# Layer 2 attention: head outputs in two halves of a PSUM bank, output products two runs later, projection weights in two buffers

## The chip, the cores and the metric

The kernel runs on one core of a Trainium2 chip. The metric is the device time of one execution in microseconds, the median of three runs. The profile is of one further execution, which has a time of its own.

## The reference

A stack of four layers works on x of shape (4, 256, 256) with a context of shape (4, 1601, 256), in float32. Each layer adds an attention part and a feed-forward part to x. The change is in the attention of layer 2, grouped-query attention with 16 query heads and 4 key/value heads of 128 values, over 1601 context positions and, causally, the 256 own ones:

```python
q = rms_norm((x @ wq).reshape(B, L, 16, 128), q_norm_w)
k = rms_norm((x @ wk).reshape(B, L, 4, 128), k_norm_w)
v = (x @ wv).reshape(B, L, 4, 128)
k_ctx = rms_norm((h_ctx_kv @ wk_ctx).reshape(B, T, 4, 128), k_norm_w)
v_ctx = (h_ctx_kv @ wv_ctx).reshape(B, T, 4, 128)
q = q * cos + rotate_half(q) * sin
k = k * cos + rotate_half(k) * sin
# keys and values: context first, then own; each repeated for 4 heads
scores = einsum('bhld,bhmd->bhlm', q, k_full) / sqrt(128) + mask
out = einsum('bhlm,bmhd->blhd', softmax(scores), v_full)
return out.reshape(B, L, 16 * 128) @ wo
```

It is applied to the layer-normalised x, and its result is added to x.

## The kernel before

The four layers run one after the other on one core. Work of a later stage is filled into gaps of an earlier one: the context's keys and values of layer 2 do not depend on x, and are computed ahead by a generator, `l2_early`. It makes products (L1307), copies them out of PSUM on ScalarE (L1314, L1315), normalises the keys on GpSimd (L1332), turns them with TensorE transposes (L1341), and stores them to DRAM (L1316 for values, L1344 for keys). `self.fill(n)` takes n steps of this generator; what is left when the attention's own preparation is through is run off by `for _ in self.early`.

`l2_xattn` works in 16 **units**: 4 batch entries times 4 key/value heads, each unit with 4 query heads, so 64 heads in all. For each unit, `prep` is a generator of small steps: on the first unit of a batch entry the layer norm and its transposes (`turned`, tile `tp_ln`, L1420); then the query products of the first 128 rows (`tpq`); the loads of the context's keys and values (kT, va) from DRAM, and the products for own keys and values (`tpkv`); the query products of the other 128 rows; the norms; the transposes of the queries (`tpqT`, L1526); and the transposes of the own keys (`tpk`, L1531), copied into kT (L1534). All these PSUM tiles have the tag "tp" in the pool `ps`, which has one buffer, so that each must be read before the next is written.

The weights of a unit, `wq` (128 x 1024 values a unit) and `wks` (128 x 512), are loaded by `load` (L1439), and its output weights `wo` (128 x 1024) by `load_out` (L1444); the loads are issued on the queue of SyncE (SP), in program order, together with those of keys and values and the early stores. `one` is a pool with one buffer for each tile, `two` has two.

The main loop counts **runs** x, 16 in a unit and 4 in a head, and takes three at a time (`pos` 0, 1, 2). A run is one of four chunks of a head: 16 score matmuls (L117, tile s), the mask and the maximum on VectorE (L1568, L1571), and the exponentials on ScalarE (L1576). The scores of three runs are issued together. Twelve runs later than its scores, a chunk of the value products of a head is done (`value_chunk`): a quarter of the 15 key tiles, accumulated in the PSUM tile `o2`, which `ps_o` holds with one buffer. After the last chunk of a head, ScalarE copies `o2` into `at` (L1631). Meanwhile the probabilities have been merged (`merge`), scaled on GpSimd (L1611) and turned on VectorE (L1617).

`beside(n, k)` says what else stands behind run k of unit n: the steps of the preparation of the next unit (k = 1, 3, 7, 9, 12) and of the one after it (k = 15, and k = 13 too where that one begins a new batch entry), the loads of weights (k = 3) and of output weights (k = 12), and `project` at k = 11. `project` does the output products of the unit before: 8 matmuls of `at` with `wo` into the PSUM tile `acc2` (tag "tp"), which show as 16 records, and VectorE adds the result to x (L1639). Its fourth head's value products have just ended at k = 11, since they come twelve runs late.

In this loop the order on TensorE is that of the program: `self.strict` pins each matmul behind the one before. The order on the other engines is largely that in which the program issues the work. An instruction waits for the semaphores of the tiles that it reads or overwrites.

Of the kernel before, what the change touches and what calls it, by code (L numbers as in the profile page):

```python
# [11 lines left out]
F32 = mybir.dt.float32  # L12
# [12 lines left out]
P = 128  # L25
B = 4
S = 256
# [22 lines left out]
REGS = 4  # L50
F1 = [1, 2, 2, 3]
G1 = [7, 4, 4, 3, 2, 2, 2, 2, 2, 2, 0]
LN2, Q2, C2 = 2, 2, 6
FIRST3 = [7, 1, 3]
EARLY = B * NKV2
NH3, HD3 = 32, 8
# [41 lines left out]
class Kernel:  # L98
# [1262 lines left out]
    def l2_xattn(self):  # L1361
# [10 lines left out]
        with ExitStack() as es:  # L1372
            one = es.enter_context(tc.tile_pool(name="a2one", bufs=1, reuse_waits="tile"))
            two = es.enter_context(tc.tile_pool(name="a2", bufs=2, reuse_waits="tile"))
            ps_s = es.enter_context(tc.tile_pool(name="a2s", bufs=3, space=PSUM))
            ps = es.enter_context(tc.tile_pool(name="a2p", bufs=1, space=PSUM))
            ps_o = es.enter_context(tc.tile_pool(name="a2o", bufs=1, space=PSUM))
# [57 lines left out]
            def load(g):  # L1435
                w = {}
                for n, shape in (("wq", [P, 2, 512]), ("wks", [P, 2, 256])):
                    w[n] = one.tile(shape, F32, name=n)
                    nc.sync.dma_start(w[n], i["l2_" + n][g])  # L1439
                return w  # L1440

            def load_out(g):
                t = two.tile([P, 4, D], F32, name="wo")
                nc.sync.dma_start(t, i["l2_wo"][g])  # L1444
                return t
# [176 lines left out]
            def values(va, pT, at, h, o, ms):  # L1622
                for m in ms:
                    n0 = {13: 1, 14: 5}.get(m, 0)
                    rows = 96 if m == 14 else P
                    self.mm(
                        o[:, 32 * n0 :].rearrange("p (n i) -> p n i", i=32), va[:rows, m, :],
                        pT[:rows, n0:, m, :], m == 0, m == CT,
                    )
                if ms[-1] == CT:  # L1630
                    nc.scalar.copy(at[:, h, :], o)  # L1631

            def project(hd):
                b, at, wo = hd["b"], hd["at"], hd["wo"]
                acc = ps.tile([P, 2, D], F32, name="acc2", tag="tp")
                for q in range(2):
                    for h in range(4):
                        self.mm(acc[:, q, :], at[:, h, q * P : (q + 1) * P], wo[:, h, :], h == 0, h == 3)
                nc.vector.tensor_tensor(self.x[b], self.x[b], acc, ALU.add)  # L1639

            ORDER = [0, 13, 14, *range(1, NM)]
            CHUNK = [ORDER[0:4], ORDER[4:8], ORDER[8:12], ORDER[12:]]

            def value_chunk(hd, n):
                if n == 0:
                    hd["o"] = ps_o.tile([P, S], F32, name="o2")
                values(hd["va"], hd["pT"], hd["at"], hd["h"], hd["o"], CHUNK[n])

            units = [(b, g) for b in range(B) for g in range(NKV2)]
            w = load(0)  # L1650
            wo = load_out(0)
            results = {0: []}
            for n, _ in enumerate(prep(0, w, results[0])):
                self.fill(Q2 if n == 0 else C2 if n == 3 else 0)
            for _ in self.early:
                pass
            w = load(1)
            self.es2.close()
            main = es.enter_context(tc.tile_pool(name="a2main", bufs=2, side="right", reuse_waits="tile"))

# [12 lines left out]
            def prepare(n):  # L1673

                if n < len(units):
                    if n not in pieces:
                        pieces[n] = prep(n, w, results.setdefault(n, []))
                    next(pieces[n], None)

            def beside(n, k):  # L1680

                nonlocal w, wo
                if k == 11 and n:
                    project(heads[4 * n - 1])
                if k in (1, 3, 7, 9) or (n, k) == (0, 0):
                    prepare(n + 1)
                if k == 12:
                    for _ in range(2):
                        prepare(n + 1)
                    if n + 1 < len(units):  # L1690
                        wo = load_out(units[n + 1][1])
                if k == 3 and n + 2 < len(units):
                    w = load(units[n + 2][1])
                if k == 15 or (k == 13 and (n + 2) % NKV2 == 0):
                    prepare(n + 2)
# [13 lines left out]
            for x0 in range(0, ALL + LATE, 3):  # L1709
                made, norms = [], False  # L1710
                for x in range(x0, min(x0 + 3, ALL)):
                    if x % 16 == 0:
                        begin(x // 16)
                    hd = heads[x // 4]
# [14 lines left out]
                for pos in range(3):  # L1729
                    x = x0 + pos  # L1730
                    if LATE <= x < ALL + LATE:
                        value_chunk(heads[(x - LATE) // 4], (x - LATE) % 4)
                    if pos == 0:
                        soften(made[2:])
                    if x < ALL:
                        beside(x // 16, x % 16)
                        norms |= x % 16 == 4
                    if pos == 0:
                        for hd in turning:
                            turns(hd)  # L1740
# [768 lines left out]
```

## Time and profile before

| what | value |
| --- | --- |
| median of 3 runs | 2410.82 us (2408.73 to 2413.48) |
| the profiled execution: its time | 2415.17 us |
| the profiled execution: span on the core | 2413.5 us |
| mean granted TensorE clock | 0.969 |
| first score matmul of layer 2 | 701.06 us |
| last output copy of a head, L1631 | 1709.8 us |

Times in the trace are microseconds from the start of the span. PE is TensorE, PEld its loading of weights, DVE is VectorE, ACT ScalarE, POOL GpSimd and SP SyncE, which only issues transfers; SPq is its queue. A row of a group names the source line, the engine, the operation, output <- inputs, the shapes and the number of instructions, and then the busy time, the mean of one in ns, and the idle time of the engine just before them with what ended most of it. A row of the timeline gives the start, the duration, and the instruction with its number; idle time before it stands in brackets, with what released it. Matmul ends are modelled, so that chains of matmuls overlap by some 0.16 us.

### The profile page before, as it was taken

To read this page: it belongs to the slowest core of one execution; us is meant where nothing else is said; L and a number is where in the kernel's file an instruction comes from. 1 tells how busy PE (TensorE), PEld (TensorE's weight loads), DVE (VectorE), ACT (ScalarE), POOL (GpSimd) and SP (SyncE) were. 2 spreads that over 40 slices of the span, in tenths; PEclk is the share of its full clock that TensorE was granted. 3 is DMA by queue.
4 is the path that set the end of the run, shared out by engine and by line. 5 is a ranking of instruction groups with operands and counts; after the bars stand their busy time and mean duration, and the time that the engine had idled before them with its cause. 6 is when DMAs were issued, how large, how long until landed. Compare 5 with 4: busy or idle time off the path is not lost.

```text
span 2413.5 us, 42181 instructions
## 1 busy us (share of the span) xinstructions
PE 2249.5 (93%) x14322; PEld 1389.0 (58%) x14335; DVE 1506.1 (62%) x3586; ACT 1267.4 (53%) x2871; POOL 950.4 (39%) x1707
## 2 busy tenths in 40 slices
PE   8989997899978999999999999999899889999996
PEld 5677875777744655555555555555765533444332
DVE  5453532673457877887877878878434484758344
ACT  3234443452455545554555545554232477888994
POOL 1014654502325554554555455455112244334220
PEclk9999998889999999999999999999899999999998
DMA  7164575652541111111111111100434254434320
GB/s 264 41 199 158 169 152 151 201 185 64 165 167 37 51 42 51 51 48 49 51 51 51 51 50 38 51 23 1 196 112 128 86 167 119 101 100 99 84 63 19
DMA packets 156078, 234.47 MB, mean 97 GB/s; under 512 B 33929, under 2 KB 122761, under 8 KB 154666
## 3 DMA queue, kind: packets, MB, share of 16 engines
q1 hardware_dynamic: 138998, 190.07, 24.8%
q0 software_dynamic: 11280, 31.60, 5.4%
q10 hardware_dynamic: 5588, 10.09, 1.4%
q8 instruction: 117, 1.92, 0.3%
q14 instruction: 95, 0.78, 0.1%
HBM read 169.94 MB, written 61.74 MB: 96 GB/s over the span
## 4 chain that ended last, share of the span: by engine, by line
PE 65%; DVE 18%; ACT 6%; issue 6%; DMA 2%; POOL 2%; SPq 0%; another core or an unknown queue 0%; ACTq 0%; PEld 0%; POOLq 0%; DVEq 0%; PEldq 0%
PE o L117 11%; PE s L117 10%; PE o L77 7%; DVE pT L1617 4%; PE b L77 3%; DVE nmsm L1571 3%; PE f2gu L117 3%; ACT p L1576 3%; PE s L77 3%; PE f1gu L117 2%; PE f0gu L117 2%; PE fill L1307 2%; PE acc L117 2%; PE av L117 2%; PE f0y L117 2%
## 5 line engine op out<-in xcount | busy, mean ns | idle before, releaser
L1576 ACT ACTIVATE p<-s,nmsm 128x448 f32<-128x448 f32 (+2 forms) x512 | 323.5, 638 | 347.2 <-DVE nmsm L1571 205.8
L117 PE MATMUL o<-pT,va 128*128 128x256 f32 (+2 forms) x1920 | 433.4, 376 | 14.0 <-ACT at L1631 13.0
L77 ACT ACTIVATE e<-s 128x1024 f32<-128x1024 f32 (+1 forms) x416 | 392.3, 1042 | 58.6 <-PE s L77 57.6
L117 PEld LDWEIGHTS o<-pT,va 128*128 128x128 f32 (+1 forms) x1920 | 345.1, 190 | 126.2 <-issue 64.9
L117 PE MATMUL s<-kT,qT 128*32 128x448 f32 (+2 forms) x4096 | 414.3, 552 | 2.6 <-ACT p L1576 2.6
L1611 POOL TENSOR_SCALAR p<-p,rm 128x448 f32<-128x448 f32 (+2 forms) x512 | 321.8, 651 | 6.3
L1571 DVE TENSOR_REDUCE nmsm<-s 128x1 f32<-128x448 f32 (+4 forms) x384 | 298.8, 785 | 7.4 <-DVE s L1568 0.2
L1617 DVE STREAM_TRANSPOSE pT<-p 128x448 f32<-128x448 f32 (+4 forms) x384 | 275.7, 773 | 4.9 <-POOL p L1611 4.9
L117 PEld LDWEIGHTS s<-kT,qT 128*32 128x32 f32 x4096 | 124.5, 110 | 251.4 <-issue 227.5
L77 PE MATMUL o<-e,va 128*32 128x512 f32 x1656 | 248.0, 617 | 14.1 <-DVE os L77 12.2
L77 PEld LDWEIGHTS s<-qb,kb 32*128 32x128 f32 (+1 forms) x1664 | 65.6, 181 | 182.5 <-issue 143.0
L1568 DVE TENSOR_TENSOR s<-s,mask 128x64 f32<-128x64 f32 (+4 forms) x384 | 92.5, 255 | 93.3 <-PE s L117 61.8
L1604 POOL TENSOR_TENSOR rm<-em,tot 32x8 f32<-32x8 f32 x256 | 50.1, 196 | 227.1 <-DVE tot L1601 205.7
L522 POOL DMA_INDIRECT f0xr<-f0xd,f0src x95 | 90.8, 955 | 69.0 <-PE f0gu L117 17.4
L1307 PE MATMUL fill<-wkc_early,ctxT 128*128 128x256 f32 (+1 forms) x444 | 109.5, 398 | 6.8 <-ACT va_early L1315 4.1
L77 PE MATMUL s<-qb,kb 32*128 32x256 f32 (+1 forms) x1664 | 111.5, 331 | 2.6 <-ACT e L77 1.8
L77 POOL CAST kb<-kf 128x384 fp32r<-128x384 f32 (+1 forms) x126 | 65.6, 549 | 97.8 <-PE s L77 51.1
L1576 ACT ACTIVATION_READ_ACCUMULATOR p<-s,nmsm 128x1 f32 x512 | 101.5, 198 | 0.0
L1307 PEld LDWEIGHTS fill<-wkc_early,ctxT 128*128 128x128 f32 (+1 forms) x444 | 86.1, 198 | 22.4 <-ACT va_early L1315 5.2
L1326 DVE TENSOR_REDUCE ss_early<-sq_early 128x4 f32<-128x512 f32 x64 | 37.2, 581 | 85.0 <-ACT sq_early L1325 65.4
L630 POOL DMA_INDIRECT f0yt<-f0yd,f0slot x64 | 62.3, 974 | 62.3 <-DVE x L622 30.7
L117 PE MATMUL f2gu<-f2wgu,f2xsT 128*128 x176 | 84.3, 603 | 0.9 <-issue 0.6
(579 smaller groups left out, 3733.9 us busy)
## 6 DMA issues: line engine op xcount, KB each, us to landing
kf<-kd SPq DMA_DIRECT2D x384, 48.0 KB
vd<-va_early SPq DMA_DIRECT2D x96, 128.0 KB
kd<-kT_early SPq DMA_DIRECT2D x48, 256.0 KB
kT<-kd SPq DMA_DIRECT2D x16, 768.0 KB
va<-vd SPq DMA_DIRECT2D x16, 768.0 KB
kd<-kt SPq DMA_DIRECT2D x96, 128.0 KB
f0yd<-f0ys SPq DMA_DIRECT2D x95, 128.0 KB
ctxT<-in_ctxT SPq DMA_DIRECT2D x5, 1664.0 KB
```

The source lines that it names most:

```text
L77: ins = f(*a, **kw)
L117: self.ordered(self.nc.tensor.matmul(out, lhsT, rhs, start=start, stop=stop, **kw))
L522: nc.gpsimd.indirect_dma_start(out=t, out_offset=None, in_=xd[:, :], in_offset=bass.IndirectOffsetOnAxis(ap=src[:, n : n + 1], axis=0),)
L630: nc.gpsimd.indirect_dma_start(out=yt, out_offset=None, in_=yd[:, :], in_offset=bass.IndirectOffsetOnAxis(ap=slot[:, t, r : r + 1], axis=0),)
L1307: ins = nc.tensor.matmul(tp[:rows, t, :], ctxT[u // NKV2][:, k, c0 : c0 + rows], w[u % NKV2][:, k, :], start=k == 0, stop=k == 1,)
L1326: nc.vector.tensor_reduce(ss[:, m0:m1], sq[:, : m1 - m0, :], AX.X, ALU.add)
L1568: nc.vector.tensor_tensor(sv, sv, mask[:, e0:e1, : nt - CT, :].rearrange("p n t i -> p n (t i)"), ALU.add)
L1571: nc.vector.tensor_reduce(ms[:, 0, e0:e1], s[:, n0:n1, : nt * 32], AX.X, ALU.max, negate=True)
L1576: nc.scalar.activation(p[:, n, : nt * 32], s[:, n, : nt * 32], AF.Exp, bias=ms[:, 0, e : e + 1], accum_out=ms[:, 1, e : e + 1],)
L1604: nc.gpsimd.tensor_tensor(r[32 * a : 32 * a + 32], e[:, a], tot, ALU.mult)
L1611: nc.gpsimd.tensor_scalar(p[:, n, : nt * 32], p[:, n, : nt * 32], r[:, e : e + 1], 1.0, ALU.mult, ALU.mult)
L1617: self.pin(nc.vector.transpose(pT[:, 2 * c + n0 : 2 * c + n1, :nt, :].rearrange("p n t i -> p n (t i)"), p[:, n0:n1, : nt * 32],))
```

## The change

There are three parts.

1. The tile `o2` is allocated once, with room for two heads (128 x 2 x 256 values, 2 KB in each partition), and successive heads use its two halves in turn. Before, each head allocated a tile of 128 x 256 from the pool of one buffer.
2. `project` is called at k = 13, no longer at k = 11: two runs later.
3. `wq` and `wks` come from the pool with two buffers. With it the start of the layer is rewritten: the weights of the second unit are loaded right after the first step of the first preparation, ahead of the output weights, where they were loaded after all of the early work. The fill steps between the steps of the first preparation are 2, 1, 1, 0, 4; they were 2 after the first and 6 after the fourth.

```diff
-LN2, Q2, C2 = 2, 2, 6
+LN2, Q2 = 2, [2, 1, 1, 0, 4]
...
                 for n, shape in (("wq", [P, 2, 512]), ("wks", [P, 2, 256])):
-                    w[n] = one.tile(shape, F32, name=n)
+                    w[n] = two.tile(shape, F32, name=n)
                     nc.sync.dma_start(w[n], i["l2_" + n][g])
...
+            results = {}
+
             def value_chunk(hd, n):
                 if n == 0:
-                    hd["o"] = ps_o.tile([P, S], F32, name="o2")
+                    hd["o"] = outs[:, hd["h"] % 2, :]
                 values(hd["va"], hd["pT"], hd["at"], hd["h"], hd["o"], CHUNK[n])
 
             units = [(b, g) for b in range(B) for g in range(NKV2)]
+            outs = ps_o.tile([P, 2, S], F32, name="o2")
             w = load(0)
+            first = prep(0, w, results.setdefault(0, []))
+            next(first)
+            w = load(1)
             wo = load_out(0)
-            results = {0: []}
-            for n, _ in enumerate(prep(0, w, results[0])):
-                self.fill(Q2 if n == 0 else C2 if n == 3 else 0)
+            for n in Q2:
+                self.fill(n)
+                next(first)
+            for _ in first:
+                pass
             for _ in self.early:
                 pass
-            w = load(1)
             self.es2.close()
...
             def beside(n, k):
 
                 nonlocal w, wo
-                if k == 11 and n:
+                if k == 13 and n:
                     project(heads[4 * n - 1])
```

## The prediction

> **What bounds the kernel now.** I read the busy times first, then the stretches of this layer, then who waits for the lines that the change touches, then the timeline at two places.
>
> ```profile
> span 2413.5 us, 42181 instructions
> PE 2249.5 (93%) x14322; PEld 1389.0 (58%) x14335; DVE 1506.1 (62%) x3586; ACT 1267.4 (53%) x2871; POOL 950.4 (39%) x1707
> L117 PE MATMUL o<-pT,va 128*128 128x256 f32 (+2 forms) x1920 | 433.4, 376 | 14.0 <-ACT at L1631 13.0
> ```
>
> The next view has, by stretch: us, then the busy time of PE, PEld, DVE, ACT and POOL, the granted TensorE clock, the DMA share, GB/s.
>
> ```profile
> 660.00:701.00 41.00, 27.61 (x129) 20.11 (x127) 27.16 (x82) 23.40 (x58) 15.01 (x18) 0.94 0.62 207
> 747.00:1713.00 966.00, 946.61 (x6410) 571.50 (x6410) 757.98 (x1591) 482.77 (x1353) 490.77 (x1088) 1.00 0.13 43
> ```
>
> The 64 heads of this layer are worked off between 747 and 1713, and there TensorE is busy for 946.6 of 966 us: any TensorE idle time added or removed there is added to or taken from the end. The stretch from 660 to 701 is the start of the layer: 41.0 less 27.6 us leaves 13.4 us of idle TensorE. Next, who waits for the copy of a head's output out of PSUM (L1631):
>
> ```profile
>   PE o L117: 13.0, 15
>   PE acc L117: 3.2, 4
> ```
>
> So 13.0 us are lost by 15 heads' first value products and 3.2 us by 4 output products. The timeline shows what else stands around that copy:
>
> ```profile
> 804.71 1.46 PE L117 MATMUL acc<-wo,at 128*128 128x256 f32 x6
> 806.96 2.43 PE L117 MATMUL acc<-wo,at 128*128 128x256 f32 x10 [0.80 <-ACT at L1631]
> 809.23 1.63 PE L117 MATMUL o<-pT,va 128*128 128x256 f32 x8
> ...
> 866.45 3.62 PE L117 MATMUL acc<-wo,at 128*128 128x256 f32 x16
> 869.90 1.63 PE L117 MATMUL o<-pT,va 128*128 128x256 f32 x8
> 873.49 0.44 PE L1531 MATMUL tpk<-ident,ko 128*128 128x128 f32 x2 [1.95 <-DVE x L1639]
> 873.85 6.53 PE L117 MATMUL s<-kT,qT 128*32 128x448 f32 x48
> ```
>
> The output products (acc, 16 records a unit) stand exactly between a head's last value product and the next head's first. They are work to do while ScalarE copies: heads 0 to 2 of a unit are read first, only the fourth waits.
>
> **The change part by part.** (1) *Halves of one bank.* The wait of 13.0 us would go if a head's first product no longer needed the copy of the head before. But both halves are parts of one tile in one 2 KB bank, and in the changed program as built the first value product of every head still waits for the ScalarE copy of the head just before it. At the unit boundaries, where it waited for acc alone, it now names that copy as well. I take 0 for the 16.2 us; the bound below is −16.2, the bound above is 0 by itself.
>
> The trace alone, one buffer and a wait of 0.4 to 1.6 us each, would let one think that the wait is about the same bytes, and would give −13.0. [...]
>
> (2) *Output products two runs later* (k 11 to 13). This moves 15 groups of 16 matmul records and with each the VectorE addition L1639; no DMA is issued by it. A group takes 869.90 − 866.45 = 3.45 us. In its new place it does the same work, but the copy it covered is bare. The runs go in threes, so the 15 units m fall into classes:
> - m = 1, 4, 10, 13: the copy ends 2.03 us after the last product (by its rows, 804.87 to 806.91 at m = 1), ScalarE being in exponentials. Before: 809.23 − 804.87 = 4.36 us from the last product of one head to the first of the next, acc included. After: 2.08 of waiting, and 3.45 elsewhere, 5.53: +1.17 each, +4.7. If the copy came at once, as in the next class, +2.5.
> - m = 2, 5, 8, 11, 14, and 7: the copy ends 0.41 us after. Before 869.90 − 866.62 = 3.28; after 0.45 + 3.45 = 3.90: +0.62 each, +3.7 for six.
> - m = 3, 6, 9, 12, 15: 48 score matmuls (some 4.8 us) stand there too and cover the copy of 0.41: 0. Without them 0.62 each.
>
> In its new place acc has the same PSUM slots ("tp") as what comes next. At m = 2, 6, 10 that is now the normalised input's transposes (tp_ln), directly after it; they must wait for L1639. That addition ends 0.72 us after acc when VectorE is free: 0.77 plus the overlap of 0.16 that a chain of matmuls has, +0.93 each, +2.8. Where VectorE is behind, as at m = 2 before (870.07 to 873.43), it is 3.36. Gone is the wait of 1.95 that the K transposes (tpk) have there: −2.1 with the overlap. Behind acc now waits tpk's copy to SBUF (0.3 to 1.3 us after tpk); 8 value products of 1.63 us stand between: 0. The addition comes two runs later on VectorE, ahead of the same transposes of probabilities, with 4 us to spare: 0. The wo load of the next unit waits for acc and starts some 4 us later on SP, where nothing is queued behind it for long; it is needed 16 runs later (60 us): 0.
>
> *Clock.* After the 1.95 us stall the granted clock reads 0.50 from 874 to 877, and the 48 score matmuls took 6.53 us against 4.77 at 752.23: −1.8 if that stall goes. After a stall of 1.58 us (from 1044.8) the clock reads 1.00. The four bare stalls of 2.08 lie beyond the row with the drop: between 0 and 4 × 1.8 = +7.2. One row is thin evidence, and I take half, +3.6.
>
> [...]
>
> Steady part: 4.7 + 3.7 + 2.8 − 2.1 − 1.8 + 3.6 = **+10.9 us**.
>
> (3) *Weights in two buffers, fills 2, 1, 1, 0, 4.* In the steady part it removes no wait, since a weight load is issued some twelve runs ahead already (issued at 685, used at 713): 0. At the start:
>
> ```profile
> 626.63 0.38 SPq L1439 DMA_DIRECT2D wq<-in_l_wq  x1
> 670.58 0.38 SPq L1444 DMA_DIRECT2D wo<-in_l_wo  x1
> 663.81 1.10 PE L1307 MATMUL fill<-wkc_early,ctxT 128*96 128x256 f32 x4 [2.55 <-ACT va_early L1315]
> 677.63 1.97 PE L117 MATMUL tpkv<-wks,xT 128*128 128x256 f32 x8 [3.38 <-issue]
> 697.81 3.33 PE L1341 MATMUL fill<-ident,kr_early 128*128 128x128 f32 x13 [3.52 <-POOL kr_early L1332]
> ```
>
> On SP the first two weight loads (768 KB) go from 626–629 to about 670, behind a store that waits for ScalarE, and the second two come up to them from 684: five loads in a row (wq and wo of 128 x 1024 f32, wks of half that: 2 MB), at the 241 and 287 GB/s of the windows 696–700 and 704–708 some 8 us, and the K and V loads are queued behind. On TensorE the first query product moves behind 13 transposes and 16 fill records, from 667.25 to 672–674, and the K/V product from 677.6 to 679–681: a loss of 0 to 3.6. The last two fill groups of products come ahead of the query transposes (1.26 us and a wait of 1.21 no longer precede them): the 3.52 us wait for POOL's normalised K ends up to 2.4 us earlier, and with 768 KB less under way at 626–650 the waits of 2.55 and 0.97 near 664 may go. Bounds −5.9 to +3.6; I take −1.5, since the wait at 697.8 ends last there.
>
> **Sum:** +10.9 − 1.5 = +9.4. On the profiled span, 2413.5 + 9.4 = 2422.9, and with the 1.7 us around it 2424.6. That run was 4.35 us above the median of three: **2420 us**.
>
> **The rivals.**
> - *Faster by the start.* Place: 660 to 701, with 13.4 us idle and a granted clock of 0.54 to 0.61 from 696 to 704 (8 us at some 0.6: 3 us). If all of it went and no stall cost clock, 7.3 − 16.4 = −9.1: 2402. It decides once the start gains over 12 (7.3 + 4.8), and over 16 with two drops. For it: less traffic, earlier products. Against it: the query chain becomes later, not earlier, and five loads now meet at 670. 0.08.
> - *The halves free the products*, and the built wait is met early: −16.2; without a wait part 2 costs only its tp_ln and tpk terms (2.8 − 2.1 − 1.8 = −1.1) and the start −1.5: 2410.8 − 18.8 = 2392. For it: the 13.0 us that L1631 holds up. Against it: the wait is in the program. 0.04.
> - *Nothing to be seen*: no clock drop at the stalls (+7.3), a start nearer its bound (−5): 2410.8 + 2.3 = 2413. For it: only one stall of this length was seen with a drop; against it: both would have to come together. 0.20.
> - *Forecast*: 0.68, its own range 2415.6 to 2429; the top has all four drops and the start at its worst (14.5 + 3.6 = 18.1: 2429).
>
> Under 0.2% (4.8 us) a measurement of this kernel can't be told from no change. Faster 0.12, same 0.20, slower 0.68. Range 2409 to 2429: it holds the forecast and nearly all of the third case, and leaves out the first two.
>
> **What would show it.** Right: the first value products wait for the copy in some 25 heads, about 24 us in all (13.0 + 4 × 2.08 + 6 × 0.45); acc waits no longer for it; gaps of about 2.08 at m = 1, 4, 10, 13; tp_ln waits on L1639 three times; the stall at 873 is gone; 747 to 1713 becomes 8 to 12 us longer. Wrong: value products that no longer wait for L1631, a start of the scores before 695, or clock readings of 1.00 behind all the 2.08 us stalls.

## The result, and the profile after

| | before | after |
| --- | --- | --- |
| median, us (6 runs each) | 2408.72 (2406.92 to 2413.48) | 2420.05 (2414.96 to 2421.10) |
| profiled execution, span, us | 2413.5 | 2418.2 |
| first score matmul of layer 2, us | 701.06 | 693.38 |
| last value product, us | 1709.74 | 1718.38 |
| the loop between them, us | 1008.68 | 1025.00 |
| idle TensorE in the loop, us | 29.66 | 41.68 |

The changed kernel is slower: the ratio is 1.0042 with a 95% interval of 1.0029 to 1.0054, 11.3 us on the medians.

The busy row and the row of the value products on the page of after:

```profile
span 2418.2 us, 42254 instructions
PE 2253.0 (93%) x14335; PEld 1389.2 (57%) x14335; DVE 1508.3 (62%) x3586; ACT 1266.7 (52%) x2871; POOL 947.1 (39%) x1707
...
L117 PE MATMUL o<-pT,va 128*128 128x256 f32 (+2 forms) x1920 | 438.6, 378 | 27.5 <-ACT at L1631 26.5
```

The value products' idle time behind the copy L1631 has gone from 13.0 to 26.5 us. Who waits for that copy (first line), and who waits for the addition L1639 (second):

```profile
  PE o L117: 26.5, 25
```

```profile
  PE tp_ln L1420: 3.2, 3
```

It is 25 heads where it was 15, the output products no longer stand in that list, and the transposes of the normalised input wait three times for the addition. The timeline of the two places shown of before:

```profile
795.95 1.56 PE L117 MATMUL o<-pT,va 128*128 128x256 f32 x6
799.55 1.74 PE L117 MATMUL o<-pT,va 128*128 128x256 f32 x8 [2.04 <-ACT at L1631]
801.13 0.38 PE L1531 MATMUL tpk<-ident,ko 128*128 128x128 f32 x2
801.34 1.89 PE L117 MATMUL o<-pT,va 128*128 128x256 f32 x8
803.07 3.62 PE L117 MATMUL acc<-wo,at 128*128 128x256 f32 x16
...
861.76 1.74 PE L117 MATMUL o<-pT,va 128*128 128x256 f32 x8 [0.46 <-ACT at L1631]
863.33 0.38 PE L1531 MATMUL tpk<-ident,ko 128*128 128x128 f32 x2
863.64 4.88 PE L117 MATMUL s<-kT,qT 128*32 128x448 f32 x48
868.45 1.99 PE L117 MATMUL o<-pT,va 128*128 128x256 f32 x8
870.28 3.62 PE L117 MATMUL acc<-wo,at 128*128 128x256 f32 x16
874.68 0.65 PE L1420 MATMUL tp_ln<-ident,xn 128*128 128x128 f32 x4 [0.78 <-DVE x L1639]
```

Between the two groups of value products (o) there is nothing but the stall now, 2.04 us at the first place and 0.46 at the second. The 16 records of acc stand behind value products that would have run anyway. The wait of tpk at the second place is gone, and tp_ln has one instead.

The start needs care. This row is the same early transpose, in layer 1's work, before and after:

```profile
635.62 0.27 PE L1341 MATMUL fillg<-ident,kr_early 128*128 128x128 f32 x1
```

```profile
629.97 0.27 PE L1341 MATMUL fillg<-ident,kr_early 128*128 128x128 f32 x1
```

The profiled execution of before was 5.65 us later already there, where both kernels do the same. By the first value product of layer 2, near 745 us, the distance is 7.34, and 7.34 − 5.65 = 1.7 us. But the distance was 7.57 already at the first transposes of layer 2's normalised input (660.66 us before, 653.09 after), which stand ahead of all that the change moves on TensorE, and it is 7.68 at the first score. Of these 1.9 us, 1.4 are waits of TensorE near 649 us that a second profile of the kernel before (below) does not have. This pair of profiles therefore shows no gain of the start that could be put down to the change; the runs with part 3 do.

### The profile page after: what moved, and what is told of

Same layout as the page of the kernel before. It is cut to its first block, busy times and chain, and to the rows that moved or that the text cites. A ratio compares the mean times of both kernels' runs of the same rounds, so it can differ in the third digit from the quotient of the medians.

```text
span 2418.2 us, 42254 instructions
## 1 busy us (share of the span) xinstructions
PE 2253.0 (93%) x14335; PEld 1389.2 (57%) x14335; DVE 1508.3 (62%) x3586; ACT 1266.7 (52%) x2871; POOL 947.1 (39%) x1707
## 4 chain that ended last, share of the span: by engine, by line
PE 45%; DVE 16%; ACT 5%; issue 3%; POOL 1%; DMA 1%; SPq 0%; PEld 0%; ACTq 0%; POOLq 0%; PEldq 0%; DVEq 0%
PE o L117 11%; PE s L117 10%; PE o L77 7%; DVE pT L1617 5%; PE b L77 4%; DVE nmsm L1571 4%; ACT p L1576 3%; PE s L77 3%; PE f2gu L117 3%; PE acc L117 2%; PE tpq L117 1%; PE f2y L117 1%; DVE s L1568 1%; DVE em L1594 1%; PE tpkv L117 1%
## 5 line engine op out<-in xcount | busy, mean ns | idle before, releaser
L117 PE MATMUL o<-pT,va 128*128 128x256 f32 (+2 forms) x1920 | 438.6, 378 | 27.5 <-ACT at L1631 26.5
```

The source lines that it names most:

```text
L117: self.ordered(self.nc.tensor.matmul(out, lhsT, rhs, start=start, stop=stop, **kw))
```

## The experiments

They ran on three chips, on each beside the kernel before; only ratios to the kernel before on the same chip are compared. "Loop" is from the first score matmul of layer 2 to the last value product.

**The kernel before once more.** No edit.

> The kernel before, unchanged, for a second profile. Theory: the profile of before was of a run that lost 5.65 us to the profile after already at 638 us, in stages where the two programs are the same; another profile of before should be 4 to 7 us shorter there (scores of layer 2 start near 695), and have the same waits in the loop: 15 heads waiting 13.0 us, 4 output products waiting 3.2 us, and the loop from first score to last output copy 1009 us. Rival: the start is that slow in every run of before, and the change made it faster: scores start again at 701.

Measured: span 2363.2 us; scores from 653.4; 15 heads wait 14.1 us, five output products 4.1; loop 1010.7. This run does the stages before layer 2 some 48 us faster, so the question of the start is not settled by this run: the expected 695 was missed, for a reason that has nothing to do with the change. The loop can be compared, and differs by 2.0 us from the first profile's 1008.7: one run of before and another of it are that far apart. In particular the copy that the output products of unit 7 wait for came at once in the first profile and late in this one. Who waits for L1631, and the output products of unit 7:

```profile
  PE o L117: 14.1, 15
  PE acc L117: 4.1, 5
...
1136.95 2.42 PE L117 MATMUL acc<-wo,at 128*128 128x256 f32 x10 [1.05 <-ACT at L1631]
```

**Output products at 13, alone.**

```diff
-                if k == 11 and n:
+                if k == 13 and n:
                     project(heads[4 * n - 1])
```

> Only the output products two runs later. Theory: this part alone makes nearly all of the loop's 16 us: first value products wait 26 us instead of 13.0, the transposes of the normalised input wait 3 us, the loop is 1024 to 1026 us long, time 12 to 16 us above before, ratio 1.005 to 1.0065. Rival (the halves make the wait longer, and this part costs less than forecast): under 8 us above before.

Measured: ratio 1.0067 (1.0052 to 1.0082), 2381.06 against 2365.26 us, +15.8 us; loop 1027.15. Who waits for L1631:

```profile
  PE o L117: 26.5, 25
```

The same 25 heads and the same 26.5 us as with the whole change. The second part alone makes the whole loss, and more.

**Halves and part 3, output products at 11.** The changed kernel with this put back:

```diff
-                if k == 13 and n:
+                if k == 11 and n:
                     project(heads[4 * n - 1])
```

> The changed kernel with the output products back at k = 11: halves and two buffers alone. Theory: waits in the loop as before (13.0 and 3.2 us), start 1.7 us earlier, time 0 to 4 us under before, ratio 0.998 to 1.000. Rival (the halves cost by themselves, since they tie the first value product to the copy at the unit boundaries): 4 to 8 us above before. Rival (the halves free the value products once the output products stand where they did): 12 us or more under before.

**Part 3 alone.** As the last, and a tile for each head again:

```diff
-                    hd["o"] = outs[:, hd["h"] % 2, :]
+                    hd["o"] = ps_o.tile([P, S], F32, name="o2")
...
-            outs = ps_o.tile([P, 2, S], F32, name="o2")
```

> Two buffers for the projection weights and the new start alone. Theory: start 1.7 us earlier, loop unchanged at 1009 us, time 0 to 4 us under before, the same as with the halves within 1 us. Rival (part 3 shifts ScalarE against TensorE in the loop, and the loop becomes 3 to 5 us longer): above before.

Measured: with halves 0.9987 (0.9978 to 0.9996), 2362.57 us; without 0.9985 (0.9974 to 0.9995), 2362.76. Who waits for L1631, with halves and then without:

```profile
  PE o L117: 14.1, 15
  PE acc L117: 3.8, 5
```

```profile
  PE o L117: 14.1, 15
  PE acc L117: 3.7, 5
```

The two lists are alike, and like that of before (14.1 and 4.1). The halves do nothing, in either direction: loops 1010.58 and 1010.29. Part 3 makes the kernel 2.5 us faster (1.2 to 6.1 by the interval), at the start: from the first transposes of the normalised input to the first score it takes 3.7 us less with halves and 2.9 without than in the second profile of before. Some 1.7 of that is one fall of the clock. Before, the key and value products of the first unit wait 3.37 us in this second profile and 3.38 in the first, and then took 3.63 us in the second, at a clock of 0.54, and 1.97 in the first, at 1.00; with part 3 they do not wait.

**Copies that do not read PSUM.** The kernel before, with:

```diff
-                    nc.scalar.copy(at[:, h, :], o)
+                    nc.scalar.copy(at[:, h, :], self.x[0].rearrange("p q d -> p (q d)")[:, :S])
```

> The kernel before, with ScalarE's copy of a head's output reading a tile of x in place of the PSUM tile: the head outputs are left out of the result, and no value product waits for a copy. All instructions keep their number, engine and size. Theory: the copy is the one wait at the head boundaries, so that its 14.1 and 4.1 us of waits go, and with 20 breaks fewer some 3 us of lost overlap: 17 to 22 us under before, ratio 0.991 to 0.993. Rival (what stands behind the wait, VectorE's transposed probabilities, is late too and takes its place): less than 8 us under before.

Measured: ratio 0.9924 (0.9908 to 0.9939), 2342.09 against 2360.89, −18.8 us; loop 990.8, idle 15.2. The value products' row on its page:

```profile
L117 PE MATMUL o<-pT,va 128*128 128x256 f32 (+2 forms) x1920 | 432.2, 375 | 2.3 <-DVE pT L1617 2.1
```

Nothing takes the wait's place. Some 19 us is thus a bound for what freedom from the copy could be worth. A second buffer for `o2` would give less, since the output products have to wait for the copy of their fourth head in any case; here they do not (4.1 us in the second profile of before). Two buffers were not run.

**Output products at 14.** As at 13, with `k == 14`.

> Output products three runs later (k = 14) in place of two, nothing else changed from before. Theory: the copies are bare as at 13 (25 heads waiting 26 us), but the normalised input's transposes no longer stand right behind the output products, so that their 3.2 us wait goes: 2 to 5 us under the run with 13, 11 to 14 above before. Rival (the price at 13 comes from the work that stands around k = 13, not from the bare head boundary): under 6 us above before.

Measured: 1.0058 (1.0044 to 1.0072), +13.7 us; loop 1020.7.

```profile
PE o L117 <- ACT at L1631: 24.9, 25, 2.4
```

No tp_ln waits; in one unit the output products wait 2.81 us for the copy of the normalised input. The bare boundary is the price at both places; the 2 us between 13 and 14 lie within the two intervals.

**Output products in halves, at two boundaries.** The core of the edit (the weights of a unit are kept by unit, and loaded at k = 8):

```diff
-            def project(hd):
-                b, at, wo = hd["b"], hd["at"], hd["wo"]
-                acc = ps.tile([P, 2, D], F32, name="acc2", tag="tp")
-                for q in range(2):
-                    for h in range(4):
-                        self.mm(acc[:, q, :], at[:, h, q * P : (q + 1) * P], wo[:, h, :], h == 0, h == 3)
-                nc.vector.tensor_tensor(self.x[b], self.x[b], acc, ALU.add)
+            def project(hd, q):
+                b, at, wo = hd["b"], hd["at"], wos[hd["n"]]
+                acc = ps.tile([P, D], F32, name="acc2", tag="tp")
+                for h in range(4):
+                    self.mm(acc, at[:, h, q * P : (q + 1) * P], wo[:, h, :], h == 0, h == 3)
+                nc.vector.tensor_tensor(self.x[b][:, q, :], self.x[b][:, q, :], acc, ALU.add)
...
-                    project(heads[4 * n - 1])
-                if k in (1, 3, 7, 9) or (n, k) == (0, 0):
+                    project(heads[4 * n - 1], 0)
+                if k == 7 and n > 1:
+                    project(heads[4 * n - 5], 1)
+                if k in (1, 3, 6, 9) or (n, k) == (0, 0):
```

> The output products in two halves of 8 records: rows 0 to 127 at k = 11 as before, rows 128 to 255 at k = 7 of the next unit, another head boundary; the transposes of the queries move from k = 7 to k = 6, output weights are loaded at k = 8. Theory (what counts is what stands at a head boundary while ScalarE copies): the waits of 0.8 to 1.6 us at k = 7 are covered by 1.7 us of products, value products wait under 5 us in place of 14.1, time 5 to 10 us under before. Rival (the halves' additions on VectorE and the one PSUM slot bring new waits of 0.5 to 1 us in each unit, and the query transposes at k = 6 wait for GpSimd): same as before or slower.

> As the run before it, but with the transposes of the queries at k = 8 and 10, after the half at k = 7. Theory: the half at k = 7 finds the PSUM slot free and covers the copy; the query transposes one run later wait for the addition less than 0.5 us, the half at k = 11 waits for the copy of the transposes at 10 some 0.5 to 1 us in a unit: 2 to 8 us under before. Rival: the slot's waits take it all, 0 to 10 us above before.

Measured: with the query transposes at 6 and 9, 0.9974 (0.9959 to 0.9990), −7.8 us; with 8 and 10, 0.9947 (0.9933 to 0.9961), −13.0 us. In the first the heads wait 2.1 us, but the output products wait 8.9 us, eight times, for the copy of the query transposes, which now stands right before them:

```profile
PE acc L117 <- ACT qT L1527: 8.9, 8, 1.2
```

In the second, who waits for L1631:

```profile
  PE o L117: 3.5, 9
```

Loop 994.5 us, idle 17.2, near to the 990.8 and 15.2 of the run whose copies do not read PSUM; on the medians it is 13.0 of that run's 18.8 us. It did better than was expected of it.

**The query transposes at 8 and 10, alone.** The kernel before, with `k in (1, 3, 8, 10)`.

> The kernel before with only the query transposes moved from k = 7 and 9 to k = 8 and 10; output products whole at k = 11. Theory (the cover at the boundary is what gained in the split): the boundary at k = 7 loses the 0.6 us of transposes that stood there, the waits of value products grow from 14.1 to 18 us or more, and the output products at k = 11 wait for the copy of the transposes at k = 10: 2 to 10 us above before. Rival (the place of the transposes gained, not the half): 5 us or more under before.

Measured: 1.0037 (1.0023 to 1.0052), +10.0 us.

```profile
  PE o L117: 18.0, 15
  PE acc L117: 1.8, 5
```

The place of the transposes is a loss by itself, so the gain is that of the split. In the trace of the split no value product of units 2 to 14 waits over 0.3 us; here nine do, each behind k = 7, by 1.24 to 2.02 us. The loop is 9.8 us longer than in the second profile of before, but only 2.3 of it is idle time. Five stalls of 1.58 have become 2.01, and behind one of them and one of 2.69 us the clock falls, some 3.3 us by the price found below; the rest of the busy time was not taken apart. The output products did not wait for the copy of the transposes, as had been thought.

**Part 3 and the split.** Both edits.

> Part 3 of the change (two buffers, new start) with the output products split into halves at k = 11 and at k = 7 of the next unit, query transposes at k = 8 and 10: the two things that were faster, together. Theory: they act in different stretches and add up: 13 to 17 us under before, ratio 0.993 to 0.9945. Rival: the later query transposes or the SP queue take back the gain at the start: the same as the split alone, ratio 0.9947.

Measured: 0.9928 (0.9913 to 0.9944), 2393.10 against 2410.51 us; loop 991.75. It has the lowest ratio of the kernels that compute everything. It gains 17.4 us where the split alone gained 13.0 and part 3 alone 2.5, but its interval and that of the split overlap, so that the two parts add up is not shown.

**The clock behind the stalls.** Output products at 13 again, and the same with work in five stalls:

```diff
                 if k == 13 and n:
                     project(heads[4 * n - 1])
+                if k == 11 and n % 3 == 1:
+                    tp = ps.tile([P, 4, P], F32, name="tpd", tag="tp")
+                    for h in range(4):
+                        self.ordered(nc.tensor.transpose(tp[:, h, :], self.ident, self.ident))
```

> The second part alone once more (output products at k = 13), on this chip, to be set beside the run with work put into its stalls: 14 to 18 us above before, five stalls of 2.03 us, behind some of which the clock reads 0.55 to 0.75.

> The second part alone, with four transposes of the identity into an unread tile at k = 11 of units 1, 4, 7, 10 and 13, where the stalls of 2.03 us are: TensorE has 0.5 us of work more in the first part of each, which changes no other wait. Theory (the clock halves behind such a stall in about half the cases, and costs 1.8 us each time): stalls of 1.6 us, clock 1.00 behind all of them, 3 to 8 us under the same kernel without the transposes. Rival (the clock readings are no cost of the stall): within 1 us of it.

Measured: 1.0067 (1.0053 to 1.0080), 2425.33 us, 14.8 above before, without the added work; 1.0062 (1.0046 to 1.0078), 2426.14 us, with it. On the time nothing is to be seen, against the expectation of 3 to 8 us. The trace shows it. These are windows without the added work, and then with it (us, busy time of PE, PEld, DVE, ACT and POOL, granted clock, DMA share, GB/s):

```profile
995.00:998.00 3.00, 2.51 (x8) 2.17 (x9) 2.93 (x7) 2.30 (x9) 0.45 (x3) 0.61 0.60 236
...
1379.00:1382.00 3.00, 3.00 (x11) 2.39 (x10) 2.72 (x4) 0.37 (x1) 0.00 (x0) 0.60 0.00 0
```

```profile
995.00:998.00 3.00, 2.01 (x11) 1.83 (x12) 2.93 (x6) 2.82 (x11) 0.76 (x4) 1.00 0.67 263
...
1379.00:1382.00 3.00, 3.00 (x15) 2.65 (x14) 1.58 (x2) 0.00 (x0) 0.00 (x0) 1.00 0.00 0
```

One of the stalls without the added work, and the same with it:

```profile
1377.06 2.38 PE L117 MATMUL o<-pT,va 128*128 128x256 f32 x8 [2.08 <-ACT at L1631]
...
1373.67 0.60 PE L1688 MATMUL tpd<-ident 128*128 128x128 f32 x4
1375.92 1.74 PE L117 MATMUL o<-pT,va 128*128 128x256 f32 x8 [1.65 <-ACT at L1631]
```

Without the work the stalls last 2.08 to 2.10 us, and behind two of five the clock falls. With it they last 1.65 and it never falls. Units 4 and 10 become 1.67 us shorter each (63.13 to 61.46 and 64.56 to 62.90), units 1, 7 and 13 stay within 0.01. The loops are 1024.7 and 1021.0; they differ also in units without added work, by −1.2 in unit 0 and +0.9 in unit 14. So a drop costs 1.67 us, and two of them are less than these medians can tell apart.

## Why the prediction was right, and where its terms were off

The forecast was slower, 2420 us, and 2420.05 was measured. The direction and the mechanism are shown; that the numbers meet to a tenth is partly luck, as the terms show.

- **Halves: 0.** Right, and shown by the two runs with and without them. The reason given, the wait that stays in the program, agrees with the trace of after: value products still wait for the copy of the head before. No run here lets these products go ahead of that copy while it reads the other half, so whether they need to wait for it is not shown. Nor does a trace show the bank that the forecast names; the argument rests on the wait.
- **Output products moved: +4.7 and +3.7 for bare copies.** The mechanism is right: 25 heads in place of 15, stalls of 2.04 and 0.46 where 2.08 and 0.45 were forecast. The class of late copies was mis-sized: it has five units, not four. Unit 7 was put among the early ones since its copy came at once in the profile of before; the second profile of before has it late too. It became 2.30 us longer where 0.62 was forecast, and 0.98 longer against the second profile. Units 1 and 8 came to 1.23 and 0.68 (1.17 and 0.62).
- **tp_ln: +2.8.** Mis-sized: 3.2 us of waits with 0.16 of overlap lost at each of three are 3.7; at unit 6 the wait was 1.64, as VectorE was late: its addition ended 1.58 us after the products, where the forecast had named 3.36 for such a case.
- **tpk: −2.1, and −1.8 of clock behind it.** The wait is gone. The clock was no part of it to be counted on: the second profile of before has the same stall (1.93 us) with a clock of 1.00 behind it. Unit 2 became 1.29 us shorter, not 2.35; its wait at k = 7 was 1.57 us after and 1.19 before, and the same difference goes with 0.8 us in units 11 and 14 (below). Against the second profile, where that wait is 1.58, it is 0.43 shorter, near to the −0.55 of the terms without the clock (0.62 + 0.93 − 2.1).
- **Clock drops: half of four, +3.6.** Two of five in the profile of after, at 1.67 each 3.3. This is the term that I took at half from a single row. That such a stall costs clock in some cases and not in others is shown by two windows of after, and its price by the two last runs:

```profile
990.00:993.00 3.00, 3.00 (x9) 2.45 (x10) 3.00 (x6) 1.77 (x6) 0.00 (x0) 0.53 0.51 203
1182.00:1185.00 3.00, 2.91 (x16) 2.63 (x17) 3.00 (x6) 2.27 (x8) 0.12 (x1) 1.00 0.57 229
```

  These are the same stalls of 2.04 and 2.03 us in the profile of after, with and without the drop.
- **Steady part: +10.9.** Measured +16.3 between the two first profiles, +14.3 against the second profile of before: the term was too small, and the loop lies outside the 8 to 12 us that the forecast named as a sign of being right. Of the 5.4 that were missing, 1.7 is unit 7, 0.9 tp_ln in unit 6, 1.1 unit 2, and 0.9 each units 11 and 14. In units 2, 11 and 14 the waits at k = 7 were 1.19 us in the first profile of before and are 1.58 in its second; units 11 and 14 are 0.8 longer there too, so that this is nearly all not of the change. Unit 5 went the other way by 1.1, with a wait at k = 7 of 1.18 in place of 1.58. The remaining 1.0 lies in differences of 0.5 and less.
- **Start: −1.5.** Measured −2.5 on the medians of part 3 alone; the first pair of profiles shows none of it. The forecast named scores that start before 695 us as a sign of being wrong, and they started at 693.38: as 5.65 of the 7.68 us were there at 635 already, this sign said little here. The five loads do stand together on SP after the change:

```profile
662.00 0.38 SPq L1439 DMA_DIRECT2D wq<-in_l_wq  x1
662.43 0.44 SPq L1439 DMA_DIRECT2D wks<-in_l_wks  x1
662.92 0.42 SPq L1439 DMA_DIRECT2D wq<-in_l_wq  x1
663.39 0.43 SPq L1439 DMA_DIRECT2D wks<-in_l_wks  x1
663.87 0.44 SPq L1444 DMA_DIRECT2D wo<-in_l_wo  x1
```

  No wait of TensorE between 655 and 700 us is put down to them or to another transfer. The wait for the normalised keys did not shrink (3.69 us in place of 3.52); it came earlier.
- **The sum.** The two-part result is 15.8 − 2.5 = 13.3 us by the single parts, and 11.3 (7 to 13 by the interval) for the whole. The forecast of 9.4 is under both; the median of before moved down by 2.1 us with three more runs, and this closed the gap.

The rivals: the halves that free the products are refuted: the waits stayed. The price set on the waits, 16.2 us, was near to the 18.8 that the run without the PSUM read gained. A start that outweighs the loop would have needed 12 us, and gained 2.5. "Nothing to be seen" is excluded by the interval.

What stays open: after the loop the trace of after gains 3.9 us on that of before in work that is the same (it is 8.6 us behind at the end of the loop and 4.7 at the end of the span), in several steps. With part 2 alone the distance is 16.5 us at the end of the loop and 16.1 at the end, so it is taken for a difference between runs.

## What to carry to other kernels

Work that stood between the last write of the accumulator and the next head's first write paid twice in this kernel, as work and as cover: with it moved away 25 heads waited 26.5 us for the copy, where 15 had waited 14.1 in the second profile of before. Before moving such work, measure the copy that it hides at every place, and over more than one profile. To get rid of such a wait, count which boundaries are bare and give each of them a share: half of the output products at each of two boundaries was worth 13 us with the query transposes after them, and 8 with these before them, where moving all of them away cost 16. In this program two halves of one tile were one buffer: the first value product in one half still waited for the copy of the other, and 15 heads waited 14.1 us for it, with the halves as without.

## What the runs showed of the hardware

The granted clock fell behind TensorE stalls of some 2 us, and not each time: behind 11 of the 24 stalls of 2.01 to 2.2 us. Over the layer-2 loops of all 14 profiles of this case, by the length of the TensorE stall and the clock in the 4 us after it:

| stall, us | stalls | with a clock under 0.95 behind |
| --- | --- | --- |
| 0.7 to 1.7 | 185 | 0 |
| 1.91 to 1.95 | 4 | 1 |
| 2.01 to 2.2 | 24 | 11 |
| 2.2 to 2.9 | 22 | 13 |
| 4.2 to 4.6 | 14 | 14 |

The last row is one wait at the start of the loop, once in each profile, and 14 stalls of the row above it are another (11 of them with the fall); of the other 8 in that row 2 have it.

The clock fell behind one stall of 1.95 us, behind 24 of the 46 stalls of 2.0 to 2.9 us, and behind none up to 1.7. The same stall had the drop in one run and not in another: the key transposes of unit 2 waited 1.95 us in the first profile of before, with a clock of 0.57 in the 4 us after it, and 1.93 us in the second, with 1.00. What decides it no run here tested.
